# Layer 2's experts moved out of the attention loop, over the tokens that chose them

## The chip, the cores and the metric

The kernel runs on one core of a Trainium2 chip. Its time is the device time of one execution in microseconds, lower is better. Before the change the median of four runs is 3542.0 us (3536.94 to 3548.18).

## The reference, cut to what matters

Four layers, each a cross attention block and a feed-forward block with a residual around each, on x of 16 sequences of 256 tokens and 256 channels in float32. Layer 2's feed-forward block is what the change touches:

```python
x = x + L2_xattn(ctx, layernorm(x), kmask)
y = layernorm(x)                               # goes into L2_ffn
h = rms(y, n1_w); q, k = rms per head; v       # 16 heads of 16, causal
ao = causal_attention(q, k, v) @ wo.T;  ao[:, :, :64] = 0
y = y + ao
xf = rms(y, n2_w)
topv, topi = top_k(softmax(xf @ gate_w.T), 2)  # 4 experts, 2 for each token
topv = topv / (topv.sum() + 1e-8)
o0 = gelu(xf @ e0_up.T) @ e0_down.T
o1 = silu(xf @ e1_w1.T) * (xf @ e1_w2.T) @ e1_down.T
o2 = gelu(gelu(gelu(xf @ e2_l1.T) @ e2_l2.T) @ e2_l3.T) @ e2_l4.T
o3 = gelu(gelu(xf @ e3_down.T) @ e3_up.T) @ e3_out.T
moe = sum over the experts of weight * o;  moe[:, :, :64] = 0
x = x + (y + moe)
```

The hidden width is 512 (256 in e3_down). An expert's output counts only for the tokens that have it among their two.

## The kernel before, in words

The kernel walks the four layers one after the other. Layer 0 is a software-pipelined loop over 16 batches (a batch is one sequence), then experts over fixed slots of 512 tokens. Layer 1 is a gather loop, a shared expert and blocks of 256 tokens that belong to one expert each. Layer 2 is one pipelined loop that holds everything: cross attention, causal self-attention, routing, and all four experts over all tokens. Layer 3 is a pipelined loop with a cross attention and at its end a quantized product.

In the three pipelined loops the order of the work is written by hand, for TensorE (PE), VectorE (DVE), ScalarE (ACT) and GpSimd (POOL): a list `order` of entries (position, function, lag, arguments). At step s each entry is called, in order of position, for batch s - lag. All four engines take their instructions in this order, so an instruction that waits holds what stands behind it on its own engine. The DMA queue of SyncE (SP) is not ordered by the list; indirect DMAs (gathers and scatters by row numbers) are issued by POOL.

Layer 2's loop, for one batch b, with lines of the profile. `x_fetch` (L1212) gathers layer 1's expert outputs, `x_sum`, `x_norm` and `x_queries` make the queries; the cross attention is an object `Heads32` with `maxima` (scores on PE L223, maxima on DVE L305), `exps` (PE L242 and L245, four exponentials on ACT L252), `added` (POOL L338 adds the two key halves of the exponentials, to halve the sums on PE), `values` (PE L347, then reciprocal L355 and product L356 on DVE). `x_back` (L1239) adds to x; `statistics`, `norm`, `turned`, `project` (L1271, L1274), `head_squares` (L1286), `head_scale` (L1294) and `heads_q`, `heads_k` (L270, through transposes) make the inputs of the self-attention. `maxima` (PE L1308 for the causal mask and L223, DVE L1318) ends what a batch does in its own step. In the next step come `exps` (L245, ACT L252, then POOL L1327 sets to zero what the causal mask excludes), `values` (L261), `back` (L1344), `out_project` (L1357), `experts_in`, `gates` (L1385). One step later come `route` and `routed`, and the experts of the batch, cut in some 30 pieces that stand between the other entries of the order: `f_up` (PE L1454, two tokens' halves of 256 columns in one PSUM bank), its activations on ACT (L1466 gelu, L1471 tanh) and DVE (L1472, L1476), `f_down` (PE L1481, 192 columns), and `f_add` (DVE L1489), which adds each expert's output with a weight that is zero for tokens that did not choose it. The weights, 14 parts, are loaded anew for each batch through 7 buffers (`fetch`). PSUM has 8 banks: 4 for scores, 1 for transposes, 1 for attention outputs, 2 for experts.

Layer 3's loop does `prepare` (loads), `statistics`, `norm`, `turned`, `keys`, `vals`, `queries`, the cross attention (`maxima`, `exps`, `added`, `values` as above), `finish` (L1695) and `z_norm`. Layer 0's order has functions of its own; `load` there also zeroes DRAM buffers.

Of the kernel before, what the change touches and what calls it, by code (L numbers as in the profile page):

```python
# [19 lines left out]
P = 128  # L20
# [16 lines left out]
def tile_kernel(ctx: ExitStack, tc: tile.TileContext, a, out):  # L37
# [72 lines left out]
    yslots = keep.tile([NBLK * BLK, D], F32, name="yslots")  # L110
    idx1 = ct([P, 2, NT], "idx1", U32)
# [287 lines left out]
    with ExitStack() as l01:  # L399
# [30 lines left out]
        with ExitStack() as l0:  # L430
# [47 lines left out]
            def load(b):  # L478
# [10 lines left out]
                if 2 <= b < 6:  # L489
                    for k in range(2):  # L490
                        dma(xe[k][(b - 2) * 1024 : (b - 1) * 1024, :].rearrange("(p r) d -> p (r d)", p=P), zero)
                        if b == 2:
                            dma(ye[k][8 * CAP :, :], zero[0:1, :D])
                if 6 <= b < 6 + (NBLK * BLK + 1023) // 1024:
# [122 lines left out]
            def scatter(b, n):  # L617
# [17 lines left out]
                (0, exps, 0, 0), (1, q_stats, -2), (2, back, 1, 0), (3, maxima, -1, 1), (4, scatter, 3, 1),  # L635
                (5, back, 1, 1), (6, values, 0, 0), (7, t_stats, 1), (8, exps, 0, 1), (9, queries, -1, 0, QMs),
                (10, maxima, -1, 2), (11, slots, 2), (12, values, 0, 1), (13, t_norm, 1), (14, exps, 0, 2),
                (15, q_norm, -2), (16, scatter, 5, 4), (17, maxima, -1, 3), (18, turned, 1), (19, values, 0, 2),
                (20, queries, -2, 0, QTs), (21, exps, 0, 3), (22, router, 1), (23, maxima, -2, 0), (24, route, 1),
                (25, load, -3), (26, queries, -1, 1, QMs), (27, values, 0, 3), (28, queries, -2, 1, QTs),  # L640
                (29, scatter, 3, 2), (30, v_heads, -2),
# [476 lines left out]
    with ExitStack() as l2:  # L1118
# [6 lines left out]
        wts = t2([P, NT, 4], "wts")  # L1125


        with ExitStack() as l2a:
# [3 lines left out]
            psums(l2a, "ps2", 4, 1, 1)  # L1132
            pf2 = l2a.enter_context(tc.tile_pool(name="ps2_ffn", bufs=2, space=PSUM))
            fp = l2a.enter_context(tc.tile_pool(name="fp2", bufs=8))
# [8 lines left out]
            n2w = col(a["n2_w"], 2, "n2w", ca)  # L1143
# [17 lines left out]
            trif = ta([P, P], "trif")  # L1161
            V.memset(trif, 0.0)
            G.affine_select(trif, trif, [[-1, P]], ALU.is_ge, -MASKED, base=0, channel_multiplier=1)
            tri2 = ta([P, 2, P], "tri2", BF16)
            for i in range(2):
                V.tensor_copy(tri2[:, i, :], trif)
# [140 lines left out]
            def mask(sc, j, t):  # L1307
                T.matmul(  # L1308
                    sc[:, :, t * P : (t + 1) * P], lhsT=ident_bf, rhs=tri2,
                    start=True, stop=False, skip_group_check=True,  # L1310
                )

# [9 lines left out]
            def exps(b, u):  # L1322
                pT = pTs[b, u] = probs(u // 2, u % 2, QMs[b], KTs[b], 32, 0.0, 1.0, None, None, True)
                q0 = u % 2 * P

                for e in pT:
                    G.affine_select(  # L1327
                        e[:, :, q0 : q0 + P], e[:, :, q0 : q0 + P], [[0, 2], [1, P]], ALU.is_ge, 0.0, base=0, channel_multiplier=-1
                    )
# [21 lines left out]
            def out_project(b):  # L1351
                xn, ss = xcs.pop(b), small(2, "ss")
                hh = hhs[b, 1] = wp.tile([P, 2, D], F32, name="hh", tag="hh")
# [23 lines left out]
            def experts_in(b):  # L1377
                xfs[b] = wp.tile([P, 2, S], F32, name="xf", tag="xf")
                transposed(xfs[b], hhs.pop((b, 1)), n2w, A)

            def gates(b):
                p, xf = ptr(), xfs[b]
# [19 lines left out]

            def routed(b):

                pr, w, m = routes.pop(b), wts[:, 2 * b : 2 * b + 2, :], small(2, "rm")
# [3 lines left out]
                oh = [sm.tile([P, 2, 4], F32, name=f"oh2{k}", tag=f"oh2{k}", bufs=2) for k in range(2)]  # L1409
                m12 = [small(2, f"m12{k}", bufs=2) for k in range(2)]  # L1410
                top2(pr, 2, 4, oh, m12)
# [387 lines left out]
```

## Time and profile before

| | |
|---|---|
| median of four runs | 3542.0 us |
| profiled execution | 3548.84 us, span 3547.1 us, mean granted TensorE clock 0.928 |
| busy | PE 3149.2, DVE 1578.2, ACT 1162.8, POOL 1064.2 us |
| layer 0's loop | about 20 to 415 us |
| layer 0's experts | about 460 to 930 us |
| layer 2's loop | about 1690 us to its last store at 3059 us |
| one steady step of it | 80.7 us |
| layer 3's loop | about 3089 to 3460 us, one step 22.05 us |

The profile is one execution. Its page gives each engine's busy time, 40 equal slices of the span with the busy share in tenths and the granted TensorE clock (PEclk), and groups of instructions by line: busy time, mean duration in ns, and the engine's idle time just before them with the operation that ended most of it. PEld is the load of weights, which runs beside PE. The timeline lists instructions in order of time. L-numbers are lines of the kernel; where a helper issues the instruction, the line is the helper's.

### The profile page before, as it was taken

Reading aid. Unit: us, or ns where it says so; the run is one execution under the profiler, and the core shown is the slowest. Engines: PE = TensorE matmul, PEld = TensorE weight load, DVE = VectorE, ACT = ScalarE, POOL = GpSimd, SP = SyncE. Lnnn points to the kernel's source line nnn. Section 1 sums busy time; section 2 is a strip of 40 time slices with the busy share of each in tenths; the row PEclk is TensorE's granted clock in tenths of the full one; section 3 lists DMA queues with packets and bytes.
Section 4 is the critical chain, followed back from the end, with each engine's and each line's share of the span. In section 5 each row is a group of like instructions: output and inputs, shape, how many; then the busy total and the mean of one; then the engine's idle time right before and its main releaser. Section 6 shows DMA issues by size and latency. Waiting matters only on the chain. (4 is left out here: it accounts for less than half of the span.)

```text
span 3547.1 us, 54867 instructions
## 1 busy us (share of the span) xinstructions
PE 3149.2 (89%) x21640; PEld 2300.6 (65%) x21640; DVE 1578.2 (44%) x3920; ACT 1162.8 (33%) x2085; POOL 1064.2 (30%) x1643
## 2 busy tenths in 40 slices
PE   7999599999777489996689999999999999699983
PEld 4666366666565258885357777777777778567751
DVE  6766511100375222222445544454555542277766
ACT  3555221111122011111235545445554454122221
POOL 2455600000472600001233333333333222055552
PEclk8999799999888799997579999999999999899995
DMA  5411112221232336664013333333333223411101
GB/s 222 151 48 41 67 64 73 70 78 41 66 116 74 107 114 201 200 194 155 21 38 99 100 101 104 105 102 104 110 108 101 84 85 115 146 31 31 31 7 48
DMA packets 262132, 332.87 MB, mean 94 GB/s; under 512 B 20891, under 2 KB 214091, under 8 KB 259700
## 3 DMA queue, kind: packets, MB, share of 16 engines
q1 hardware_dynamic: 249588, 296.59, 26.2%
q0 software_dynamic: 12288, 32.78, 2.7%
q8 instruction: 171, 2.80, 0.3%
q14 instruction: 85, 0.70, 0.1%
HBM read 259.29 MB, written 70.80 MB: 93 GB/s over the span
## 5 line engine op out<-in xcount | busy, mean ns | idle before, releaser
L1454 PE MATMUL pf<-hf,fw 128*128 128x256 f32 x1280 | 302.5, 380 | 0.0
L1454 PE MATMUL pf<-xf,fw 128*128 128x256 f32 x1152 | 291.1, 390 | 0.0
L252 ACT ACTIVATE big<-pmm 128x512 f32<-128x512 f32 (+1 forms) x512 | 237.2, 549 | 124.5 <-PE pmm L245 116.1
L1454 PEld LDWEIGHTS pf<-hf,fw 128*128 128x128 f32 x1280 | 234.6, 190 | 31.8 <-issue 4.8
L1454 PEld LDWEIGHTS pf<-xf,fw 128*128 128x128 f32 x1152 | 208.0, 190 | 55.1 <-issue 27.6
L780 PE MATMUL pmm<-xiT,w 128*128 128x512 f32 x512 | 225.6, 599 | 5.5 <-DVE xiT L134 5.4
L788 PE MATMUL pacc<-w,h 128*128 128x256 f32 x1024 | 223.6, 379 | 0.0
L1327 POOL TENSOR_SCALAR_AFFINE_SELECT big<-big 128x256 f32<-128x256 f32 x256 | 105.0, 427 | 395.2 <-ACT big L252 388.4
L788 PEld LDWEIGHTS pacc<-w,h 128*128 128x128 f32 x1024 | 194.6, 190 | 33.3 <-issue 7.7
L816 POOL DMA_INDIRECT y<-ye,idx x64 | 65.2, 1019 | 479.3 <-issue 479.3
L789 DVE COPY yo<-pacc 128x256 f32<-128x256 f32 x64 | 27.2, 425 | 402.1 <-PE pacc L788 402.1
L305 DVE TENSOR_REDUCE max<-pmm 128x2 f32<-128x512 f32 x256 | 158.9, 682 | 91.6 <-PE pmm L223 91.1
L1481 PE MATMUL pf<-fw,hf 128*128 128x192 f32 x1024 | 191.2, 331 | 0.2
L1318 DVE TENSOR_REDUCE qpad<-pmm 128x2 f32<-128x256 f32 (+1 forms) x256 | 124.9, 551 | 139.7 <-PE pmm L223 139.7
L522 DVE TENSOR_REDUCE qpad<-pmm 128x2 f32<-128x512 f32 x256 | 159.0, 684 | 52.0 <-PE pmm L223 49.8
L338 POOL TENSOR_TENSOR big<-big 128x512 f32<-128x512 f32 x128 | 158.6, 1272 | 73.3 <-ACT big L252 73.2
L780 PEld LDWEIGHTS pmm<-xiT,w 128*128 128x128 f32 x512 | 96.3, 191 | 124.6 <-issue 112.4
L1481 PEld LDWEIGHTS pf<-fw,hf 128*128 128x128 f32 x1024 | 165.6, 190 | 13.7 <-issue 11.9
L1212 POOL DMA_INDIRECT y<-yslots,idx x64 | 66.7, 1042 | 319.5 <-DMA yslots<-yb 305.9
L355 DVE RECIPROCAL rT<-pacc 128x256 f32<-128x256 f32 x64 | 112.1, 1751 | 95.3 <-PE pacc L347 95.3
L1466 ACT ACTIVATE hf<-pf 128x512 f32<-128x512 f32 x176 | 104.8, 595 | 124.3 <-PE pf L1454 123.6
L146 POOL TENSOR_SCALAR rsq<-mv 128x2 f32<-128x2 f32 x128 | 25.1, 196 | 355.9 <-DVE mv L164 338.1
(383 smaller groups left out, 6213.1 us busy)
## 6 DMA issues: line engine op xcount, KB each, us to landing
w<-in_w_dram SPq DMA_DIRECT2D x16, 1024.0 KB
fw<-in_e_upT_dram SPq DMA_DIRECT2D x32, 512.0 KB
fw<-in_e_l2T_dram SPq DMA_DIRECT2D x32, 512.0 KB
fw<-in_e_l3T_dram SPq DMA_DIRECT2D x32, 512.0 KB
wg<-in_w_gate_dram SPq DMA_DIRECT2D x39, 352.0 KB
wu<-in_w_up_dram SPq DMA_DIRECT2D x39, 352.0 KB
fw<-in_e_downT_dram SPq DMA_DIRECT2D x32, 384.0 KB
wd<-in_w_down_dram SPq DMA_DIRECT2D x39, 256.0 KB
```

The lines of the kernel that those rows point to most:

```text
L252: A.activation(e[:, :, q0:], sc[j], AF.Exp, bias=bias, scale=scale)
L305: V.tensor_reduce(self.m[:, t, j, :], sc, AX.X, ALU.max, negate=True)
L338: G.tensor_tensor(r, self.pT[0][j], self.pT[1][j], ALU.add)
L355: V.reciprocal(rT, p[:, 1, :])
L522: V.tensor_reduce(qps[b][t][:, 8 * cp + j : 8 * cp + j + 5 : 4, 17], sc, AX.X, ALU.max, negate=True)
L780: T.matmul(p, lhsT=w1[:, c, f * P : (f + 1) * P], rhs=xiT[:, c, :], start=(c == 0), stop=(c == 1))
L788: T.matmul(p[:, :D], lhsT=hT[f][:, s * P : (s + 1) * P], rhs=w2[:, f, :], start=(f == 0), stop=(f == 7))
L1318: V.tensor_reduce(qp[:, 8 * cp + j : 8 * cp + j + 5 : 4, 16], sc, AX.X, ALU.max, negate=True)
L1327: G.affine_select(e[:, :, q0 : q0 + P], e[:, :, q0 : q0 + P], [[0, 2], [1, P]], ALU.is_ge, 0.0, base=0, channel_multiplier=-1)
L1454: T.matmul(p[:, j * S : (j + 1) * S], lhsT=w[:, c, f * P : (f + 1) * P], rhs=x, start=(c == 0), stop=(c == len(src) - 1),)
L1466: A.activation(f_hidden(to, f), p, AF.Gelu)
L1481: T.matmul(p[:, t * S : t * S + D - M], lhsT=hs[src][f // 2][:, f % 2, t * P : (t + 1) * P], rhs=w[:, f, :], start=(f == 0), stop=(f == 3),)
```

## The change

The experts leave layer 2's loop. In their place the loop does, for each batch: `routed` keeps the one-hot choices and the two weights; `places` counts, with two small matmuls and a running sum, at which row of its expert's region each token and choice goes; `scatter` writes the normalized token rows `hh` to these rows of a DRAM buffer `xe2` (four indirect DMAs on POOL a batch, a small memset ahead of each); `x_out` stores x without the experts' sum. After the loop each expert runs over its own region, 2048 rows in blocks of 512 (`tokens`); then, behind branches on the expert's count, over further blocks of 128, 128, 256, 512, 512 and 512 rows. The outputs go to a DRAM buffer `ye2`. Layer 3's loop gathers them (`fetch`, four indirect DMAs on POOL a batch) and adds them with their weights (`chosen`).

In the attention of layer 2, the causal mask of `exps` becomes a matmul ahead of the scores (`maskT`), instead of POOL's affine select after the exponential; the entries "added" are gone, so that `values` sums both halves on PE; scores have 5 PSUM banks instead of 4 and transposes 2 instead of 1, as the experts' 2 are free. The orders of the loops of layers 0, 2 and 3 are written anew; in layers 2 and 3, exps 0 of the cross attention moves from the start of a step to the end of the step before. Layer 0's `load` zeroes `xe2` and the upper half of each region of `ye2` as well.

```diff
+    REG = B * S
+    xe2 = keep.tile([4 * REG, D], F32, name="xe2")
+    ye2 = keep.tile([4 * REG, D - 64], F32, name="ye2")
...
+                dma(xe2[b * 1024 : (b + 1) * 1024, :].rearrange("(p r) d -> p (r d)", p=P), zero)
+                n0 = b // 4 * REG + REG // 2 + b % 4 * 512
+                dma(ye2[n0 : n0 + 512, :].rearrange("(p r) d -> p (r d)", p=P), zero[:, : 4 * (D - 64)])
...
-            psums(l2a, "ps2", 4, 1, 1)
-            pf2 = l2a.enter_context(tc.tile_pool(name="ps2_ffn", bufs=2, space=PSUM))
+            psums(l2a, "ps2", 5, 2, 1)
...
+            def maskT(sc):
+                T.matmul(sc[:, :, :P], lhsT=ident_bf, rhs=tri2[:, 1], start=True, stop=False, skip_group_check=True)
...
-                pT = pTs[b, u] = probs(u // 2, u % 2, QMs[b], KTs[b], 32, 0.0, 1.0, None, None, True)
-                q0 = u % 2 * P
-                for e in pT:
-                    G.affine_select(
-                        e[:, :, q0 : q0 + P], e[:, :, q0 : q0 + P], [[0, 2], [1, P]], ALU.is_ge, 0.0, base=0, channel_multiplier=-1
-                    )
+                pTs[b, u] = probs(u // 2, u % 2, QMs[b], KTs[b], 32, 0.0, 1.0, None, maskT, True)
...
+            def places(b):
+                oh = ohs.pop(b).rearrange("p t k e -> p (t k) e")
+                ohf = oh.rearrange("p a e -> p (a e)")
+                p = ptr()
+                T.matmul(p[:, 0:16], lhsT=before, rhs=ohf, start=True, stop=True)
+                T.matmul(p[:, 16:32], lhsT=ones, rhs=ohf, start=True, stop=True)
+                cum = sm.tile([P, 5, 4], F32, name="cumx", tag="cumx", bufs=2)
+                V.tensor_copy(cum[:, 0, :], taken[0])
+                for i in range(4):
+                    V.tensor_tensor(cum[:, i + 1, :], cum[:, i, :], p[:, 16 + 4 * i : 20 + 4 * i], ALU.add)
+                taken[0] = cum[:, 4, :]
...
+            def scatter(b, t):
+                for k in range(2):
+                    G.memset(apart, 0.0)
+                    i = G.indirect_dma_start(
+                        out=xe2, out_offset=bass.IndirectOffsetOnAxis(ap=idx2[:, k, 2 * b + t : 2 * b + t + 1], axis=0),
+                        in_=hhs[b, 1][:, t, :], in_offset=None,
+                    )
...
             order = [
+                (0, x_step, 0, "exps", 1), (1, heads_q, 1, 0, QMs), (2, gates, 2), (3, route, 2), (4, x_out, 2),
+                (5, weights, 1), (6, x_mask, -1), (7, x_step, 0, "values", 0), (8, routed, 2),
+                (9, x_step, 0, "values", 1), (10, heads_q, 1, 1, QMs), (11, exps, 1, 0), (12, x_load, -2),
+                (13, x_back, 0), (14, statistics, 0), (15, exps, 1, 1), (16, x_queries, -1), (17, x_fetch, -2, 0, 0),
+                (18, x_step, -1, "maxima", 0), (19, values, 1, 0), (20, norm, 0), (21, places, 2), (22, values, 1, 1),
+                (23, turned, 0), (24, x_step, -1, "maxima", 1), (25, x_step, -1, "split"), (26, project, 0, 0),
+                (27, x_fetch, -2, 0, 1), (28, project, 0, 1), (29, scatter, 2, 0), (30, head_squares, 0, 0),
+                (31, head_squares, 0, 1), (32, head_scale, 0), (33, exps, 1, 2), (34, exps, 1, 3),
+                (35, x_step, -1, "turned"), (36, values, 1, 2), (37, values, 1, 3), (38, heads_k, 0, 0),
+                (39, back, 1, 0), (40, back, 1, 1), (41, heads_q, 0, 0, QTs), (42, heads_k, 0, 1),
+                (43, heads_q, 0, 1, QTs), (44, maxima, 0, 0), (45, x_fetch, -2, 1, 0), (46, normed_again, 1),
+                (47, scatter, 2, 1), (48, back_turned, 1), (49, maxima, 0, 1), (50, out_project, 1), (51, maxima, 0, 2),
+                (52, maxima, 0, 3), (53, x_fetch, -2, 1, 1), (54, x_sum, -2), (55, x_norm, -2), (56, experts_in, 1),
+                (57, x_step, -1, "exps", 0),
             ]
...
+            def tokens(e, n0, n):
+                r, rows = n // P, slice(e * REG + n0, e * REG + n0 + n)
+                xi = fx.tile([P, 4, D], F32, name="xi2", tag="xi2", bufs=3)
+                dma(xi[:, :r, :], xe2[rows, :].rearrange("(p r) d -> p r d", r=r))
+                x = [fx.tile([P, 512], F32, name="xT2", tag="xT2", bufs=4) for c in range(2)]
+                for c in range(2):
+                    p = ptr()
+                    for i in range(r):
+                        T.transpose(p[:, i * P : (i + 1) * P], xi[:, i, c * P : (c + 1) * P], ident)
+                    evac(x[c][:, :n], p[:, :n], n2w[:, c : c + 1])
...
+                dma(ye2[rows, :].rearrange("(p r) d -> p r d", r=r), yo[:, :r, :])
+            share = REG // 2
+            for e in range(4):
+                for n0 in range(0, share, 512):
+                    tokens(e, n0, 512)
+            def more(e, many, n0, sizes):
+                if sizes:
+                    with tc.If(many > n0):
+                        tokens(e, n0, sizes[0])
+                        more(e, many, n0 + sizes[0], sizes[1:])
+            for e in range(4):
+                many = nc.values_load(cnt[0:1, e : e + 1], min_val=0, max_val=REG)
+                more(e, many, share, [128, 128, 256, 512, 512, 512])
...
+            (0, finish, 1, 0), (1, fetch, -4, 0, 0), (2, x_step, -1, "maxima", 0), (3, finish, 1, 1),
+            (4, x_step, 0, "exps", 1), (5, x_step, 0, "added", 1), (6, fetch, -4, 0, 1), (7, x_step, 0, "added", 2),
+            (8, x_step, 0, "added", 0), (9, x_step, 0, "added", 3), (10, statistics, -3), (11, statistics, 1),
...
+            (25, fetch, -4, 1, 1), (26, x_step, -1, "turned"), (27, vals, -2, 1), (28, mask_row, -3), (29, prepare, -4),
+            (30, chosen, -4), (31, x_step, -1, "exps", 0),
```

## The prediction

> **What bounds the kernel now.** I read the page first, its busy shares and its 40 slices.
>
> ```profile
> PE 3149.2 (89%) x21640; PEld 2300.6 (65%) x21640; DVE 1578.2 (44%) x3920; ACT 1162.8 (33%) x2085; POOL 1064.2 (30%) x1643
> PE   7999599999777489996689999999999999699983
> PEclk8999799999888799997579999999999999899995
> ```
>
> Slices 22 to 34 of 40 (about 1850 to 3000 us) are layer 2's loop: PE 9 everywhere, PEclk 9. So that stage is bound by TensorE at the full clock, and work taken off TensorE there counts if nothing takes its place. Next the windows of one steady step of this loop (80.7 us from one "turned" to the next), and of the step before experts have any token: step 1, which runs the same attention and no expert.
>
> ```profile
> 2201.50:2282.20 80.70, 79.89 (x648) 62.47 (x646) 41.35 (x112) 41.13 (x72) 27.04 (x47) 1.00 0.33 104
> 1746.70:1826.70 80.00, 63.66 (x430) 37.54 (x429) 36.03 (x79) 23.31 (x49) 27.50 (x46) 0.65 0.05 16
> ```
>
> Columns: length, busy PE, PEld, DVE, ACT, POOL, granted clock. This pair is the case in small: without experts the step took 80.0 us, no less than with them. They fill the holes of the attention, and without them the clock fell to 0.65. The timeline of step 1 shows the holes (in brackets, idle PE and what ended it):
>
> ```profile
> 1761.46 1.07 PE L347 MATMUL pacc<-big,ones 128*32 128x256 f32 x6 [2.66 <-POOL big L338]
> 1764.95 1.93 PE L347 MATMUL pacc<-big,val 128*32 128x256 f32 x16 [1.37 <-DVE uT L356]
> 1799.71 1.11 PE L270 MATMUL ptr<-ident,qpad 128*128 128x128 f32 x4 [0.78 <-ACT KT L141]
> ```
>
> They sum to about 17 us; most of the 80 is slow clock. Then the steady timeline, for true rates (start to start, since printed durations overlap):
>
> ```profile
> 2206.83 1.89 PE L1454 MATMUL pf<-hf,fw 128*128 128x256 f32 x8
> 2208.56 0.60 PE L270 MATMUL ptr<-ident,qpad 128*128 128x128 f32 x4
> 2221.49 1.46 PE L1481 MATMUL pf<-fw,hf 128*128 128x192 f32 x8
> 2222.79 0.60 PE L1308 MATMUL pmm<-tri,ident_bf 128*128 128x256 bf16 x4
> 2272.13 1.88 PE L1271 MATMUL pmm<-wqk,hT 128*128 128x512 f32 x4
> 2273.84 1.03 PE L1274 MATMUL pmm<-wvT,hT 128*128 128x256 f32 x4
> ```
>
> 256 columns cost 1.73/8 = 0.216 us, 192 columns 1.30/8 = 0.163, 512 columns 1.71/4 = 0.43: cost goes with columns, so wider blocks gain nothing on TensorE by themselves. Last the groups by shape, for the other engines' prices:
>
> ```profile
> L1327 POOL TENSOR_SCALAR_AFFINE_SELECT big<-big 128x256 f32<-128x256 f32 x236 | 96.4, 425 | 369.6 <-ACT big L252 363.5
> L1466 ACT ACT_TABLE_LOAD x59 | 75.7, 1283 | 6.5 <-PE pf L1454 5.7
> L1318 DVE TENSOR_REDUCE qpad<-pmm 128x2 f32<-128x512 f32 x112 | 69.6, 684 | 41.1 <-PE pmm L223 41.1
> L355 DVE RECIPROCAL rT<-pacc 128x256 f32<-128x256 f32 x26 | 45.6, 1754 | 49.6 <-PE pacc L347 49.6
> ```
>
> **Removed from the loop.** Per batch 152 expert matmuls of 256 columns and 64 of 192: 152 x 0.216 + 64 x 0.163 = 43.3 us of TensorE, of 80.7. ScalarE loses 11 gelus (0.595), 2 tanhs (0.613) and some 8 table loads (116 in the 1150 us of the groups, 1.283 each): 41.1 - 18.1 = 23 us left. POOL loses 16 affine selects (0.425) and 4 adds (1.275), and gains 4 scatters (as L1212's gathers, 1.05) and 4 memsets (about 0.13): 27 - 11.9 + 4.7 = 20. DVE loses f_add (8 x 0.407) and 4 x 0.681, and gains places, 11 small operations at some 0.18: 37. TensorE keeps 37.4 and gains 16 mask matmuls (4 in 0.53: 2.1) and 16 of ones32, since "added" is gone (8 in 0.54: 1.1): 41 us at full clock.
>
> **The new step.** No engine fills it, so the chain sets it: the order runs exps 1 of the cross attention (position 0) to maxima 3 (52) and exps 0 (57) of one batch in one step, and TensorE takes it in order. From the rows: exps 0 and 1 are 8 evictions on ScalarE, 0.688 each, values 0 done at 6.4; reciprocal 1.754, product 0.424, values 1 in the one pacc bank (1.8), the same DVE pair again: 13.2. x_back 0.43, add 0.69, statistics 1.2 on DVE and 3 on POOL, norm 0.9, turned, its eviction 0.94: 21.5. Two projections, 2.65 each: 26.8; their evictions, head_squares 0.69, head_scale's 12 small operations 2.9 and two products 1.15: 33. Six transposes through two banks that ScalarE or DVE drain (0.69): 37. Maxima: 8 x 0.418 + 8 x 0.684 + 0.56 on DVE: 47.3; exps 0 then: 48.3 us with all clocks full. TensorE would be busy 41/48 = 85%. What the clock does with that decides. The attention of layer 0 (100 to 400 us) is 93% busy at 0.97, the gather stage 950 to 1110 is 75% busy at 0.84, step 1 at 0.65. About 16 us of the chain are matmuls; with a sixth of the time at half clock they cost 3 more. I take 51 us a step; bounds are 41 (TensorE alone) and 80 (step 1 as it was).
>
> [...]
>
> Loop: steps 1 to 15 took 80 + 14 x 80.7 = 1210, now 15 x 51 = 765; step 0 about 7 less. Drain: 103 us from 2956 to the last store; now step 16 without new batches 28, step 17 (routing, places, four scatters in series) 20, landing and first load 10: 45 less.
>
> **Experts behind the loop.** The reference's routing gives 2366, 1754, 2006 and 2066 tokens to the four experts. 16 fixed blocks of 512: 608 matmuls at 0.43 + 512 at 0.163 = 347; transposes 16 x 0.87 = 14; the wait for xT's eviction after each block's transposes (about 0.7, as these are issued only after the block before) 11, tails 6: 378. Layer 0's experts, built alike, ran at 99% and clock 1.00 (500 to 900), so no more is added. Weights are loaded once instead of 16 times; that was hidden and counts nothing, and e2's and e3's land while e0 and e1 run (77 + 49 us of cover; without it some 20).
>
> **Branches.** Expert 0 runs 128, 128 and 256 more, expert 3 128. SP issues each load inside its branch behind the store of the body before, so bodies run in series: load 2, transposes, up, gelu, down and copy 5 to 7: 7 + 7 + 9 + 8 = 31. Counts and the entry, where each engine waits for all others, 6. About 10 jumps on TensorE's way; no row here shows a jump. Nearest are an instruction packet and a landing:
>
> ```profile
> q8 instruction: 171, 2.80, 0.3%
> 3059.39 2.01 DMA xd<-x
> ```
>
> 0.3% of 16 queues over 3547 us is 1.0 us a packet; a jump lies between 0 and 3 us; I take 1.5, as both a packet and a start are in it: 15. Sum 52, bounds 35 and 95.
>
> [...]
>
> **Layer 3.** Four gathers a step on POOL (1.05) and four multiply-adds on DVE (0.41). One gather stands between two of the adds for which values 0 waits already:
>
> ```profile
> 3318.31 4.96 POOL L338 TENSOR_TENSOR big<-big 128x512 f32<-128x512 f32 x4 [0.43 <-ACT big L252]
> 3323.32 0.62 PE L347 MATMUL pacc<-big,ones 128*32 128x256 f32 x2 [0.17 <-POOL big L338]
> ```
>
> So that wait grows by 1.0, 16 times: 16 us (0 if exps 0, now issued a step earlier, gives it back; 30 if DVE, 74% busy, also lags). The first batch gathers before its statistics: 8. Layer 0 is reordered and writes 23 MB more zeros; DMA has room (share 0.19 from 100 to 400): 0, plus or minus 8.
>
> **Sum.** -1210 + 765 - 7 - 45 + 378 + 52 + 16 + 8 = -43 us on 3548.8 (span 3547.1): 3506. The four runs have a median 6.8 lower, so I forecast 3499. Each microsecond of the step is 15; the sum is zero at 53.9.
>
> **Rivals.** *The clock takes the cover's place.* Without experts TensorE falls to half clock in the holes, as in step 1, and its 41 us stretch; above 53.9 us a step the change loses. At 58 it gives 3604, at 80 it would be 3934. For it: step 1's 0.65. Against: its transposes had one bank, its exps four, "added" made the 2.66 us hole; those are gone. *A tight loop.* The order hides more of the chain than I count, DVE (37) and TensorE (41) come near their bounds: 44 us, 3394. For it: layers 0 and 3 run 93 to 99% busy with such orders; against: one pacc bank and the serial head_scale. *A dear tail.* Branches and drain at their upper ends with the step as forecast: 3542 to 3560. The change does what it says: half the expert rows are left out by counts that the reference fixes.
>
> **Chances.** Forecast (49 to 53 us) 0.45, tight loop 0.16, clock 0.31, dear tail 0.08. Faster by over 0.2% (7 us, about what a measurement here can tell from none): 0.42 + 0.16 + 0.01 = 0.59; slower: 0.29 + 0.05 = 0.34; the rest, 0.07, within. The range reaches from 45 us a step (3409) to 59 (3619); the forecast's own case alone is 3469 to 3529.
>
> **What would show it.** Right: a step of 49 to 53 us, clock 0.85 to 0.95 in it, an expert stretch near 380 us at 1.00 without affine selects or table loads in the loop, 50 us of gappy work before layer 3, a layer 3 step near 23 us. Wrong: a loop clock under 0.75, an expert stretch over 410, or holes over 3 us at each branch.

## The result and the profile after

The changed kernel is slower by 0.4%: 3551.5 us against 3540.7 (medians of 39 and 60 runs), ratio 1.0038, 95% interval 1.0029 to 1.0048. The forecast was 3499 and "faster"; the sign was wrong. The profiled execution has a span of 3554.4 us, 7.3 more than before.

The page of the changed kernel, busy shares and slices as shown of before:

```profile
PE 2982.7 (84%) x20130; PEld 1979.7 (56%) x20130; DVE 1576.3 (44%) x3980; ACT 972.4 (27%) x1903; POOL 1019.8 (29%) x1517
PE   7999599999677399996788888888859998499983
PEclk9999799999888699997789999999979999799995
```

Layer 2's loop is now the slices 21 to 29, at PE 8 where it was 9. Then come the experts (slices 31 to 34, PE 9 and 8, 0.99 of the full clock in the windows below) and the branches with the start of layer 3 (PE 4). TensorE's busy time fell by 167 us, where the prediction's figures give 16 x (80.7 - 41) - 361 = 274 at the full clock: what is left in the loop ran more slowly (granted clock 0.91 over the 14 steps below).

The windows of the changed kernel, columns as in the prediction ("turned", from which steps are counted, is that of the cross attention: TensorE's transposes of nmp, L325 before and L331 after): the 14 steps from the second to the last "turned", one steady step, the fixed expert blocks, the branches, layer 3's loop.

```profile
1703.70:2494.60 790.90, 657.65 (x6457) 399.81 (x6455) 512.35 (x1457) 322.62 (x690) 268.39 (x458) 0.91 0.12 37
2158.40:2214.70 56.30, 46.85 (x471) 28.93 (x467) 36.95 (x107) 23.32 (x50) 20.10 (x34) 0.91 0.13 41
2624.10:2997.20 373.10, 366.20 (x1248) 213.27 (x1248) 40.85 (x64) 76.96 (x123) 0.00 (x0) 0.99 0.10 36
2997.20:3049.50 52.30, 26.55 (x122) 23.05 (x122) 3.16 (x8) 9.64 (x25) 0.00 (x0) 0.74 0.10 31
3103.60:3444.70 341.10, 325.77 (x2918) 225.48 (x2918) 265.06 (x554) 86.49 (x149) 232.50 (x262) 0.98 0.14 40
```

And of before, the same 14 steps and layer 3's loop:

```profile
1719.60:2847.00 1127.40, 1088.37 (x8660) 832.38 (x8661) 570.04 (x1521) 550.38 (x960) 366.98 (x630) 0.96 0.30 92
3110.00:3439.40 329.40, 320.70 (x2918) 223.69 (x2918) 242.83 (x501) 87.77 (x150) 182.50 (x214) 0.99 0.09 27
```

| Stretch | before | after | difference | forecast |
|---|---|---|---|---|
| start to the first "turned" of layer 2 | 1678.0 | 1668.1 | -9.9 | 0 |
| first to second "turned" (step 0) | 41.6 | 35.6 | -6.0 | -7 |
| the 14 steps to the last "turned" | 1127.4 | 790.9 | -336.5 | 14 x (51 - 80.7) = -416 |
| last "turned" to layer 3's first | 263.0 | 609.0 | +346.0 | -30 - 45 + 378 + 52 + 8 = +363 |
| layer 3's loop | 329.4 | 341.1 | +11.7 | +16 |
| to the end | 107.7 | 109.7 | +2.0 | 0 |

The differences sum to +7.3, the forecast to -44 (-43 in its own rounding). Everything but the 14 steps came out 28 us better than forecast; these came out 79 worse, 56.5 us a step over the 14 (55.6 in the steady ones) where 51 was forecast. So the question for the runs was what makes the step 55.6.

The timeline of TensorE in one step of the changed kernel, from the cross attention's exps (L248, L251) to its values (L353):

```profile
2174.59 0.51 PE L248 MATMUL pmm<-minus,sel 32*128 32x256 bf16 x2
2176.03 0.26 PE L248 MATMUL pmm<-minus,sel 32*128 32x256 bf16 x1 [0.33 <-DVE qpad L1340]
2178.04 0.28 PE L248 MATMUL pmm<-minus,sel 32*128 32x256 bf16 x1 [0.67 <-ACT big L258]
2179.20 1.24 PE L251 MATMUL pmm<-QTx,KTx 32*128 32x256 f32 x8
2183.98 1.94 PE L353 MATMUL pacc<-big,val 128*32 128x256 f32 x16
2190.06 1.07 PE L353 MATMUL pacc<-big,val 128*32 128x256 f32 x16 [2.43 <-DVE rm L1424]
```

Three things are to be seen. The same 16 matmuls of L353 take 1.94 us for values 0 and 1.07 for values 1: the first ran at half rate. The "minus" matmuls wait for a score bank (pmm), held by the maxima's reductions (qpad) and by the exps' own evictions (big); over the whole step, the stops of this kind that the timeline lists ahead of L248, L1327 and L1333 add up to 3.5 us (L1327 and L1333 are the mask's matmuls, whose inputs are constants). And values 1 waits for VectorE, whose small instructions of routed also stand ahead of values 1's own reciprocal. The half rate lasts from 2178.2 to 2188.4 (granted clock 0.50 there).

### The profile page after: what moved, and what is told of

It is laid out like the page before. It is cut to its first block, busy times and chain, and to the rows that moved or that the text cites. A ratio compares the mean times of both kernels' runs of the same rounds, so it can differ in the third digit from the quotient of the medians.

```text
span 3554.4 us, 51627 instructions
## 1 busy us (share of the span) xinstructions
PE 2982.7 (84%) x20130; PEld 1979.7 (56%) x20130; DVE 1576.3 (44%) x3980; ACT 972.4 (27%) x1903; POOL 1019.8 (29%) x1517
## 5 line engine op out<-in xcount | busy, mean ns | idle before, releaser
L825 POOL DMA_INDIRECT y<-ye,idx x64 | 65.5, 1023 | 479.2 <-issue 479.2
L1674 POOL DMA_INDIRECT y<-ye,idx x64 | 64.4, 1006 | 459.6 <-SPq L1580 446.4
L152 POOL TENSOR_SCALAR rsq<-mv 128x2 f32<-128x2 f32 x128 | 25.6, 200 | 450.6 <-DVE mv L170 444.5
L1568 DVE COPY yo<-pacc 128x384 f32<-128x384 f32 (+1 forms) x36 | 19.5, 541 | 303.7 <-PE pacc L1564 303.7
L267 PE MATMUL pacc<-big,vpad 128*32 128x256 f32 (+1 forms) x2048 | 133.0, 369 | 0.3
L229 PE MATMUL pmm<-kpad,QT 32*128 32x256 f32 x1024 | 125.4, 431 | 3.5 <-ACT big L258 1.8
L353 PE MATMUL pacc<-big,val 128*32 128x256 f32 x1024 | 91.6, 449 | 43.6 <-DVE rm L1424 33.8
L276 PE MATMUL ptr<-ident,qpad 128*128 128x128 f32 x512 | 94.8, 314 | 35.2 <-DVE qpad L179 20.3
L1545 ACT ACTIVATE h<-pmm 128x512 f32<-128x512 f32 (+2 forms) x122 | 67.4, 554 | 196.2 <-PE pmm L1538 196.0
L791 ACT ACTIVATE h<-pmm 128x512 f32<-128x512 f32 x128 | 76.4, 597 | 155.6 <-PE pmm L789 155.6
L276 PEld LDWEIGHTS ptr<-ident,qpad 128*128 128x128 f32 x512 | 61.6, 156 | 86.0 <-issue 48.9
```

The costliest lines, as they stand in the source:

```text
L229: T.matmul(sc[j][:, i, :nk], lhsT=QT[rows, c, t * P : (t + 1) * P], rhs=KT[rows, c, :nk], start=(mask is None), stop=True, skip_group_chec ...
L267: T.matmul(O[32 * j : 32 * j + 32, i, q0:], lhsT=lhsT(kc, 8 * cp + 4 * i + j), rhs=pT[j][:, i, q0:], start=(kc == 0 and i == 0), stop=(kc ...
L276: T.transpose(p[:, c, :], src[:, h0 + 4 * c : h0 + 4 * c + 4, :].rearrange("p h d -> p (h d)"), ident)
L353: T.matmul(p[32 * j : 32 * j + 32, k, :], lhsT=ones32 if k else self.val[:, kc, 32 * h : 32 * h + 32], rhs=self.sum[j][:, i, :] if k and s ...
L791: A.activation(h, p, AF.Gelu_apprx_tanh)
```

## The experiments

Two theories stood at the start. *Chain*: the step is one serial chain, and specific delays in it were left out. *Clock*: the granted clock (what grants it is "the gate" in two of the expectations) sets it, because the loop gives TensorE too little to do. A third, *engine work*, says that TensorE has more to do than was counted. The table has all runs. The step is the mean of the 14 from the second to the last "turned"; in brackets the median of the last 12 steps. The clock is that of those 14 steps. Steps and clock are of one profiled execution for each run. The ratio is to the kernel before in the same group of runs. The kernel before took 3460 us in some groups and 3545 in others; the 80 us lie ahead of layer 2 (first "turned" at 1590 or 1670), so only ratios and stretches are compared.

| Run | step, us | clock | layer 3 step | ratio [95%] |
|---|---|---|---|---|
| c_after (the changed kernel) | 55.8 (55.6) | 0.93 | 22.75 | 1.0038 [1.0026, 1.0050] |
| e1_routed | 57.1 (58.0) | 0.90 | 22.72 | 1.0078 [1.0050, 1.0106] |
| e3_between | 58.1 (57.9) | 0.88 | 22.74 | 1.0141 [1.0126, 1.0156] |
| e2_four | 66.1 (64.9) | 0.82 | 22.66 | 1.0516 [1.0500, 1.0531] |
| e2_warm | 63.1 (63.2) | 0.92 | 22.59 | 1.0371 [1.0356, 1.0387] |
| e9_six | 62.8 (63.1) | 0.86 | 22.65 | 1.0361 [1.0345, 1.0377] |
| e8_fill | 54.9 (54.6) | 0.99 | 22.66 | 0.9986 [0.9977, 0.9995] |
| e10_norm | 55.2 (54.5) | 0.98 | 22.75 | 0.9993 [0.9984, 1.0003] |
| e11_all | 55.7 (54.9) | 0.96 | 21.93 | 0.9969 [0.9958, 0.9981] |
| e12_less | 55.1 (54.6) | 0.96 | 21.96 | 0.9980 [0.9968, 0.9992] |
| e13_nofill | 56.7 (57.9) | 0.89 | 21.96 | 1.0024 [1.0010, 1.0038] |
| e14_early | 58.2 (59.1) | 0.86 | 22.67 | 1.0112 [1.0089, 1.0136] |
| e16_early_fill | 56.5 (57.2) | 0.96 | 22.68 | 1.0038 [1.0023, 1.0052] |
| e15_best | 59.3 (61.4) | 0.88 | 21.91 | 1.0200 [1.0181, 1.0219] |
| e17_all | 57.2 (56.3) | 0.91 | 21.88 | 1.0057 [1.0043, 1.0071] |
| e5_l3fetch | 55.8 (55.6) | 0.93 | 22.02 | 1.0018 [1.0001, 1.0036] |
| e18_fill_l3 | 54.7 (54.6) | 1.00 | 21.95 | 0.9950 [0.9937, 0.9964] |
| e7_before_noexp (one execution; it leaves out the experts' part of the result) | 76.5 (78.3) | 0.71 | 21.93 | - |

**The base and two changes of order.** The first is the changed kernel itself, the others move instructions.

Expected of c_after:

> The changed kernel itself, as the common base of this group of runs. All theories: layer 2's loop takes 55 to 56 us a step, and the ratio to the kernel before is 1.003 to 1.005. If the clock's windows set the step and not a chain of fixed length, a single execution may also hold stretches of steps of another length, such as the 58.0 us eight times in a row that the run with routed at 14.5 showed, and the ratio may then reach 1.01.

It came out as expected, 1.0038 again.

```diff
-(8, routed, 2),
+(14.5, routed, 2),
```

Expected of e1_routed:

> Layer 2's routed step is issued at 14.5 instead of 8, so that its small DVE instructions no longer stand ahead of the reciprocal of the cross attention's values 1. Chain theory (the step of 55.7 us is one serial chain, and routed holds it up there by the 1.2 us between the end of the values' matmuls and the reciprocal): the step falls by about 1.2 us, to 54.5, and the whole by some 19 us, to about 3533. Rival, engine work (the step grew because PE has more to do than was counted): no change within 0.1 us a step. Rival, clock (the slow stretch after the maxima sets the step, whatever DVE does): the reciprocal comes earlier, but the gain is lost again behind it, under 5 us in all.

The reciprocal did come earlier: x_back starts 15.6 us after exps 1 is issued instead of 17.3. But the stretch from there to "turned" grew from 20.3 to 23.7 us, with half rates in it. The chain theory's 1.2 us a step were lost again, and more. The last six steps are all of the same length (the expectation above miscounts them as eight); two of them:

```profile
2194.67:2252.70 58.03, 49.58 (x471) 29.80 (x467) 36.70 (x107) 23.20 (x50) 20.02 (x34) 0.88 0.13 40
2252.70:2310.73 58.03, 49.59 (x471) 29.80 (x467) 36.69 (x107) 23.32 (x50) 20.02 (x34) 0.88 0.11 35
```

The traces of before and of the changed kernel record the granted clock as 1.0 or 0.5, in 62 and 112 stretches. Each of these, the last of an execution aside, lasts a whole number of times 3.41 us, 1 to 359 times (such a length of 3.41 us is called a window here); 58.03 is 17 of them.

```diff
-(8, routed, 2), ... (10, heads_q, 1, 1, QMs), (11, exps, 1, 0),
+(14.5, routed, 2), ... (1.5, heads_q, 1, 1, QMs), (8, exps, 1, 0),
```

Expected of e3_between:

> As the run with routed at 14.5, and also the self-attention's queries (heads_q 1 of the step before) at 1.5 and its exps 0 at 8, between the values 0 and values 1 of the cross attention, so that PE has matmuls while values 1 waits for its bank and for DVE. Chain theory: exps 0 moves out of the stretch behind values 1 into a hole of 2.4 us, which takes 2 to 4 us off the step (52 to 54) and 30 to 60 us off the whole (3490 to 3520). Rival, engine work: PE's busy time is the same, so the step stays within 0.5 us of 55.7. A third way: the ACT evictions of exps 0 stand ahead of those that values 1 needs, and the step grows by 1 to 2 us.

A miss for both named theories; the third way had the sign. 57.9 us, clock 0.88. Against e1_routed, whose edit it holds, it is 1.0 us longer on the mean and no longer on the median.

**Banks, and added matmuls.** The changed loop has five banks for scores, two for transposes and one for the values.

```diff
-psums(l2a, "ps2", 5, 2, 1)
+psums(l2a, "ps2", 4, 2, 1)
```

Expected of e2_four:

> Layer 2's score banks go from 5 to 4; nothing else. It is the control for the run with added matmuls, which needs the eighth bank. Chain theory with the bank waits as one of its terms: the step grows by 0.5 to 2 us (8 to 32 us in all), since the exps of the cross attention wait for ACT to empty a bank more often. Rival, engine work: no change within 0.2 us a step.

One score bank less costs not 0.5 to 2 but some 10 us a step (7 in the next run, where added matmuls bring the clock to 0.92). That is the largest effect of any edit to the changed kernel here. The expectation of e9_six below gives 64.2 for this run; the table has 66.1. Next the same with added matmuls, which write only into the bank that came free:

```diff
+warm = ...tile([P, 512], F32, name="warm", tag="warm")
+def fill(b, n):
+    for _ in range(n):
+        T.matmul(warm, lhsT=ident_bf, rhs=tri2..., start=True, stop=True, ...)
+(49.5, fill, 0, 4), (51.5, fill, 0, 4), (52.5, fill, 0, 4), (56.5, fill, 0, 4), (0.5, fill, 1, 4), (7.5, fill, 1, 6),
```

Expected of e2_warm:

> As the run with 4 score banks, with 26 added bf16 matmuls of 128x512 a step in the eighth bank, whose results nobody reads, four or six each in the sparse maxima stretch at the step's end and at its start. They add about 26 x 0.22 = 5.5 us of PE work a step at full clock (0.22 estimated from the step's rows of bf16 matmuls of that width at full rate). Clock theory (the first 10 us of a step run at half rate because the maxima stretch before them leaves the array little to do): the matmuls of exps 1 and values 0 run at the full rate, and the step falls by 2 to 4 us against the run with 4 banks alone, although PE has more to do. Engine-work rival: the step grows by 3 to 6 us. If neither holds, the gate doesn't count this work, and the rates at the step's start stay at half.

The clock theory held: more work on TensorE, and the step fell by 3.0 us (1.7 on the median) while the clock rose from 0.82 to 0.92. Engine work as a cause is out. Then the other division of the banks, and the added matmuls with all banks kept:

```diff
-psums(l2a, "ps2", 5, 2, 1)
+psums(l2a, "ps2", 6, 1, 1)
```

Expected of e9_six:

> Six score banks and one transposes' bank in layer 2's loop, in place of five and two. The run with four and two took 64.2 us a step against 55.7. If the score banks are what the chain waits for, the sixth takes 1 to 4 us more off the step. Rival: the single bank of the transposes makes each wait for the eviction of the one before, about 0.6 us for some ten of them, and the step grows by 2 to 6 us. Clock theory: either way the step comes out near a multiple of 3.41 us.

The rival won: 62.8 us, so two banks for transposes matter as well. The split 5, 2, 1 is the best of the three.

```diff
+def fill(b, n):
+    p = pacc()
+    for _ in range(n):
+        T.matmul(p, lhsT=ident_bf, rhs=tri2..., start=True, stop=True, ...)
+(44.5, fill, 0, 4), (49.5, fill, 0, 4), (51.5, fill, 0, 4), (52.5, fill, 0, 4), (56.5, fill, 0, 4), (0.5, fill, 1, 4),
```

Expected of e8_fill:

> The changed kernel with all its banks, and 24 added bf16 matmuls of 128x512 a step, four each at six places between 44.5 and 0.5 of the order, into the bank of the values' sums, which stands free there. Nobody reads what they write. Clock theory: the stretch of exps 1 and values 0 runs at the full rate, the step falls by 2 to 4 us, to 52 to 54, and the whole by 30 to 60 us against the changed kernel, although PE has some 5 us more to do in each step. Engine-work rival: the step grows by 3 to 5 us. A third way: the clock is kept up where the work was added, and the half rate moves on into the projections, which leaves the step within 1 us of 55.7.

The windows of a step of this run, and its timeline at the place shown above:

```profile
2230.20:2284.80 54.60, 46.15 (x491) 28.92 (x490) 37.01 (x107) 23.20 (x50) 20.03 (x34) 1.00 0.12 38
```
```profile
2137.78 1.04 PE L1475 MATMUL pacc<-tri,ident_bf 128*128 128x512 bf16 x4
2139.09 1.03 PE L1475 MATMUL pacc<-tri,ident_bf 128*128 128x512 bf16 x4
2140.05 0.29 PE L248 MATMUL pmm<-minus,sel 32*128 32x256 bf16 x4
2142.09 0.26 PE L248 MATMUL pmm<-minus,sel 32*128 32x256 bf16 x1 [0.67 <-ACT big L258]
2143.25 0.71 PE L251 MATMUL pmm<-QTx,KTx 32*128 32x256 f32 x8
2146.63 1.07 PE L353 MATMUL pacc<-big,val 128*32 128x256 f32 x16
```

The clock is 1.00 and values 0 runs in 1.07 us. Yet the step is 54.6, only 1.0 less than in the changed kernel, where 2 to 4 were expected. From "turned" to exps 0 it is 19.0 us, against 16.2 in the changed kernel, since the added matmuls (L1475) stand there; from exps 0 to values 0 it is 6.6 against 9.4. What the clock gave, the added matmuls took. So at the full clock the chain lies between 54.6 - 2.8 = 51.8 and 54.6, and not at the 48.3 of the forecast. The granted clock gives the same lower end: three steady steps of the changed kernel (55.3, 55.6 and 56.3 us at 0.94, 0.94 and 0.91) hold seven windows of 3.41 us at half rate. These can have cost at most half their length, 3.98 us a step, and 55.74 - 3.98 = 51.8.

**Which term of the chain is too short?** At the full clock the segments of e8_fill stand against the forecast's: exps 0 to the end of values 0 8.5 (forecast 6.4), values 0 to x_back 6.8 (6.8), x_back to the projections 10.5 (8.3), the two projections 5.4 (5.3). Two of them are long by 2.1 and 2.2 us. The rest of the step, up to the next exps 0, is 23.4 against 21.5, and 20 of the 24 added matmuls stand in it. For the second, VectorE's timeline in e8_fill has the maxima's reductions ahead of norm (hh):

```profile
2161.05 2.48 DVE L311 TENSOR_REDUCE max<-pmm 128x2 f32<-128x512 f32 x4 [2.14 <-PE pmm L229]
2163.45 0.73 DVE L179 TENSOR_SCALAR hh<-x,mv,s 128x256 f32<-128x256 f32 x2
```

```diff
-(20, norm, 0), (21, places, 2),
+(17.5, norm, 0), (23.5, places, 2),
```

Expected of e10_norm:

> The run with the added matmuls (54.6 us a step, every matmul at the full rate), and norm at 17.5 instead of 20, ahead of the cross attention's maxima, and places at 23.5 instead of 21. Theory: at the full clock the step is a serial chain, and the forecast left out that DVE's four maxima reductions (2.49 us) stand ahead of norm's two instructions, which wait 1.6 us longer than for their own input: the step falls by 0.8 to 1.6 us, to 53.0 to 53.8. Rival (the step locks to the clock's windows of 3.41 us, of which 54.6 is 16): it stays at 54.6 or falls by a whole window to 51.2. Engine-work rival: no change, since no engine has less to do.

Nothing: 54.5 us. The same place in its timeline shows why:

```profile
2183.43 0.73 DVE L179 TENSOR_SCALAR hh<-x,mv,s 128x256 f32<-128x256 f32 x2 [2.98 <-POOL s L1266]
2186.02 0.37 PE L305 MATMUL pmm<-mb,ones_bf 1*128 1x512 bf16 x1 [0.23 <-DVE max L311]
2187.18 1.98 PE L1290 MATMUL pmm<-wqk,hT 128*128 128x512 f32 x4
```

norm now waits for its own input alone and starts 1.6 us earlier in the step (40.8 us after "turned" against 42.4). But the reductions start 1.5 us later, and the mask's matmul (L305), which stands ahead of the projections, waits for a bank that they hold. The projections start 0.3 us earlier than in e8_fill, and 0.1 of it is left at the end of the step.

Expected of e11_all:

> The same, with routed at 14.5 and layer 3's second gather behind its adds. Chain theory: now that the clock is full, the 1.2 us of DVE work ahead of values 1's reciprocal, which gave nothing at the slow clock, come off the step: 51.5 to 52.6 us a step, and layer 3 another 10 us less; in all some 40 us under the run with the added matmuls alone. Clock rival: as without the added matmuls, what is taken off comes back behind, and the step stays within 0.5 us of the run before it.

For e12_less, against e11_all:

```diff
-(52.5, fill, 0, 4), (56.5, fill, 0, 4),
+(52.5, fill, 0, 2), (56.5, fill, 0, 2),
```

Expected of e12_less:

> The same, with two instead of four added matmuls at each of the two places (52.5 and 56.5) that stand between maxima 3 and the cross attention's exps. Chain theory: 4 x 0.26 us less TensorE work on the chain, of which some is hidden behind the wait for a bank: 0.3 to 1.0 us a step less. Clock theory: if these are needed to hold the clock, half-rate matmuls return in exps 1 and values 0, and the step grows by 1 to 3 us.

Expected of e13_nofill:

> The run with all the changes of order, without any added matmul. Chain theory with the clock as a term of its own (about 4 us a step): 52 to 53 us a step, as 2 to 3 us of chain are gone, and about the time of the run with the added matmuls, which cost about as much on the chain as they save. Clock theory (what the chain loses, the gate takes back): 55 to 58 us a step, as with routed alone moved, where x_back came 1.7 us earlier and the step took 56 to 58.

None of the three is shorter than 54.6 us a step on the whole. e11_all lost the full clock (0.96) and its steps vary from 54.1 to 59.8; the two at clock 1.00 are 54.4 and 54.1, where the chain theory had 51.5 to 52.6. e12_less lost the full clock for 3.41 us in each steady step, and these are 54.6 each, 16 windows of 3.41. Of the last ten steps of e13_nofill, eight take 57.9 to 58.2 (17 windows) and two 54.7 (16). One of its early steps kept the full clock without any added matmul:

```profile
1819.34:1871.98 52.64, 43.88 (x470) 27.31 (x467) 36.21 (x104) 23.23 (x50) 18.26 (x32) 1.00 0.14 41
```

That is 1.5 to 1.8 us less than e11_all's two, which have the same order and the added matmuls, and still 4.3 over 48.3 (counted between other instructions, the step is 52.6 to 53.3). So the chain became a little shorter, but without added matmuls the run kept the full clock in this one step only.

For the first segment, exps 0 is moved ahead of maxima 3:

```diff
-(57, x_step, -1, "exps", 0),
+(51.5, x_step, -1, "exps", 0),
```

Expected of e14_early:

> The changed kernel with exps 0 of the cross attention at 51.5, between maxima 2 and maxima 3, instead of 57; nothing else. Its inputs are ready since 35. Chain theory (exps 0 to values 0 is on the chain, 2.1 us longer than forecast because of the banks): ScalarE evicts exps 0 while DVE reduces maxima 2 and 3, values 0 starts 2 to 3 us earlier after maxima 3, and the step falls to 52.5 to 54. Clock rival: the half rate moves to another place and the step comes out at 54.6 or at 58.0 (16 or 17 windows of 3.41 us). Rival on the banks: two more banks are taken between maxima 2 and maxima 3, which wait for them; what exps 0 gains maxima 3 loses, and the step stays within 0.7 us of 55.7.

Expected of e16_early_fill:

> The run with 24 added matmuls (54.6 us a step, all at the full rate) with exps 0 of the cross attention at 51.5; the four added matmuls that stood at 51.5 are at 51.2. At the full clock only the chain can answer. Chain theory: 2 to 3 us less, 51.5 to 52.6 a step. Rival on the banks: within 0.7 us of 54.6. Lock rival: exactly 54.6 again, or 51.2 (15 windows).

In e14_early the clock fell to 0.86 and the step came out at 58.2 (59.1), near the clock rival's 58.0 on the mean alone; its one step at the full clock is again shorter than those with added matmuls:

```profile
2230.72:2284.43 53.71, 43.54 (x470) 27.01 (x467) 36.79 (x107) 23.31 (x50) 20.07 (x34) 1.00 0.14 43
```

In e16_early_fill three of the 14 steps kept the full clock, and these are the test: 54.8 us, clock 1.00. Its timeline in one of them:

```profile
2233.15 0.26 PE L248 MATMUL pmm<-minus,sel 32*128 32x256 bf16 x1 [0.33 <-DVE qpad L1340]
2235.17 0.27 PE L1327 MATMUL pmm<-tri,ident_bf 128*128 128x256 bf16 x1 [0.54 <-ACT big L258]
2235.74 0.27 PE L1327 MATMUL pmm<-tri,ident_bf 128*128 128x256 bf16 x1 [0.31 <-ACT big L258]
2243.27 1.07 PE L353 MATMUL pacc<-big,val 128*32 128x256 f32 x16
```

exps 0 is done early, and now maxima 3 (L1327) waits for the banks that exps 0 holds. Values 0 starts 25.6 us after "turned" (2217.7), as in e8_fill (2146.63 - 2121.05). The rival on the banks won, on these three steps: from the maxima to the values the pace stays the same whichever stands first, and what stands second waits for the five score banks to be emptied.

Expected of e15_best:

> As the run before in this list, with 16 added matmuls a step (four each at 44.5, 49.5, 52.5 and 0.5), and layer 3's second gather behind its adds. Chain theory: the eight matmuls less are 2.1 us of TensorE work, of which at least 1 us stood on the chain, so 50.5 to 52 us a step if the clock holds; the whole about 1.5% faster than the kernel before. If the clock doesn't hold with 16, half rates come back and the step is 53 to 55.

Expected of e17_all:

> As the run before, with routed at 14.5, norm at 17.5 and places at 23.5. Chain theory: routed's 1.2 us come off the step on top (49.5 to 51), norm gives nothing by itself because the mask's matmul for the maxima then waits for a bank. Clock rival: as in the runs where routed was moved before, the gain is lost again to half rates between x_back and the projections: no less than the run before, or more.

Both missed. With 16 added matmuls the clock isn't held, 0.88 and 0.91: e15_best has three early steps of 54.83 at 1.00, no shorter than with 24, and it ends in eight steps of 61.44 us each, 18 windows of 3.41.

**The experts taken out, and nothing else.**

```diff
+work = []
...
-at_, scale = 0.5, 97.0 / sum(w[0] for w in work)
+at_, scale = 0.5, 0.0
...
-part(0, 0)
```

Expected of e7_before_noexp:

> The kernel before with layer 2's experts left out of its loop, and nothing in their place: the attention, the routing and the store of each batch in the order of before. It separates taking the experts out from writing the loop anew. The prediction read step 1 (80.0 us without experts, clock 0.65) as this loop's length without cover. If that holds, about 80 us a step, no less than with them. If step 1 was slow for a reason of its own (the loop's start), 55 to 65 us a step at a clock of 0.75 to 0.9, which is what a plain removal gives before any new order.

One step of it, from the windows:

```profile
2250.00:2328.30 78.30, 61.62 (x472) 36.95 (x465) 39.53 (x107) 24.89 (x55) 29.96 (x54) 0.71 0.08 23
```

76.5 us a step on the mean at clock 0.71: the 43.3 us of removed matmuls bring 4 us of 80.5. The other 20 us of the loop's gain come from the new order, the banks that the experts gave back, and the masks that left POOL, which were not separated. The prediction's reading of step 1 (80.0) came near, and it is what speaks most plainly against the change. Its first reading, that the stage is bound by TensorE and that work taken off it counts, was not borne out: with all of that work gone, and nothing in its place, the loop kept 95% of its time.

**Layer 3, and a version that beats both.**

```diff
-(6, fetch, -4, 0, 1),
+(9.5, fetch, -4, 0, 1),
```

Expected of e5_l3fetch:

> In layer 3, the second gather of the block four ahead (fetch -4, 0, 1) stands behind the four adds, at 9.5, instead of between the first and the second. The prediction's term for it was 1.0 us a step. If that term is right, layer 3's loop falls from 22.74 us a step by 0.6 to 1.0 us, 9 to 16 us in all. Rival: POOL's gathers don't bound the loop and the longer step comes from chosen's instructions on DVE: no change within 0.2 us a step.

The loop fell by 0.73 us a step, 11 in all: the prediction's mechanism for this stage was right, and nearly all of the stage's loss comes from that one gather.

Expected of e18_fill_l3:

> The changed kernel with the 24 added matmuls at their first places (54.6 us a step) and layer 3's second gather behind its adds (about 11 us in all), and no other change. If the terms add, as they lie in different stages: 54.6 us a step, 22.0 us a step in layer 3, ratio to the kernel before 0.995 to 0.997. If the clock falls into another pattern of windows, steps of 55 to 56 and a ratio near 1.000.

Both terms add. All 13 later steps are 54.6 us at clock 1.00. Ratio 0.9950, interval 0.9937 to 0.9964: faster than before by 0.5%, and than the changed kernel by 0.9% (0.9950/1.0038).

## Why the prediction was wrong

- **The step.** This is the step of the prediction that failed: "48.3 us with all clocks full", and with it 51. Measured at the full clock it is 54.6 with the added matmuls, at least 51.8 without; the single steps at 1.00 without them are 52.6 and 53.7, in orders slightly changed. The sum counted each instruction's duration and, for the order, who waits for whom; it counted no wait for a score bank. It named the one pacc bank and the two transposes' banks, but not the five score banks. The runs point to these as the place: one bank less costs 10 us, two moves of instructions (e10, e16) turned into waits for banks at the full clock, to within 0.3 us of the same step, and the listed waits for them are 3.5 us in the step shown of the changed kernel and 2.7 in one of e8_fill. That VectorE's reductions and ScalarE's evictions hold these banks is seen in the waits (0.33 us on qpad, 0.67 on big in the step shown). No run gave the scores a bank more without taking one from the transposes, so the length without this limit is not shown, nor that the banks account for all of the difference. The sum has slips too: its printed terms up to the end of the second DVE pair give 12.6 and not 13.2, its terms for the maxima 9.4 and not 10.3. They make the forecast longer, so the miss doesn't come from them.
- **The clock.** The allowance was 3 us; the changed kernel's clock share lies between 55.6 - 54.6 = 1.0 and 55.6 - 51.8 = 3.8. So the term was about right, and the loop's clock (0.91) is inside the forecast 0.85 to 0.95.
- **The rival "the clock takes the cover's place"** had the number (above 53.9) and half of the mechanism. The clock did fall in the sparse stretch (0.50 from 2178.2 to 2188.4 in the step shown), and 24 matmuls that compute nothing brought it back (0.99 in e8_fill). But at clock 1.00 the step is still above 53.9. What I had not priced is that the clock also hinders mending: shorter chains came out at 54.6, 58.0 or 61.4 us (e12_less, e1_routed, e15_best), 16, 17 or 18 windows.
- **Engine loads.** DVE 37, ACT 23, POOL 20 a step: measured 37.0, 23.3, 20.1. TensorE 41 at the full clock: 43.5 and 43.9 in the two steps at 1.00 without added matmuls. Near, and of little use, as no engine bounds the step.
- **Experts, branches.** 373 against 378 for the blocks, at clock 0.99; 52.3 against 52 for the branches. The other 12 of the -17 of that stretch lie in the drain and in layer 3's start, and were not followed up. In the branches the longest stop of TensorE is ahead of expert 3's body:

```profile
3038.72 0.66 PE L1532 MATMUL ptr<-ident,xi 128*128 128x128 f32 x2 [12.79 <-DMA xi<-xe]
```

  It holds, in series, the end of the body before, the jumps over the blocks that don't run, and the load; the prediction summed these one by one (2 us a load, 1.5 a jump), and how much of the stop each has was not read. No run shows a jump by itself, so its 1.5 us stays an estimate: the trace has 9.25 us from the issue of the last store before this body (3026.56) to the issue of its load (3035.81), the jumps among them, and 2.91 from there to the transposes.
- **Layer 3.** +0.78 us a step against 1.0; e5_l3fetch put 0.73 of it on the gather between the adds.
- **Ahead of layer 2.** -9.9 against 0. Kernels of this series with the same code up to there and the slower start came to the first "turned" between 1666.1 and 1675.3 us, so it may be no more than scatter; e7_before_noexp, with before's code up to there, came at 1595.9, and e18_fill_l3 in the same group at 1591.3.

With 56.5 instead of 51 in the sum, 14 steps cost 77 us more, and before's own steps were 80.5 on the mean and not 80.7 (2 us): -44 becomes +35. The 28 us that the other stretches came out better leave the measured +7. Of these 28 at least the 9.9 ahead of layer 2 and the 12 that were not followed up are no merit of the sum: that the whole missed by less than its step did is in good part luck. The profiled execution had somewhat longer early steps (61.8 and 58.5) than the base run (54.3 to 57.9), which is why its 14 steps are 56.5 and not 55.8.

## What to carry to other kernels

Price a serial step in banks as well as in instructions: count how many buffers the chain passes through, and who empties each, because the wait can move along with what is put first: in e16_early_fill exps 0 stood first, maxima 3 waited 0.54 and 0.31 us for its banks, and values 0 started 25.6 us after "turned", as in e8_fill. When dense work is taken out of a loop, look in the trace for a step that already ran without it; its length is the nearest row there is. Where the clock falls in a sparse stretch, added matmuls that write to a free bank are a cheap test of how much is the clock (e8_fill: 0.93 to 0.99, 55.8 us a step to 54.9), and sometimes worth keeping.

## What the runs showed of the hardware

All but the last of the 62 stretches of one granted clock in the trace of before, and of the 112 of the changed kernel, are whole multiples of 3.41 us. Three runs repeated a step near such a multiple: 58.03 us six times in a row in e1_routed (17.00), 61.44 eight times in e15_best (18.00), 54.6 ten times in e12_less (16.00). In e8_fill the step is 54.59, with the clock at 1.00 over the last 13 steps; that it is near 16 windows may be chance. In the changed kernel three steps together (55.3, 56.3, 55.6) make 49 windows. An edit meant to take 1.2 us off the chain cost 2.4 in e1_routed (58.0 against 55.6). The runs show the pattern; why a step repeats at such a length was not settled.

In the step shown of the changed kernel the clock fell (0.91) although TensorE was busy 46.85 of 56.3 us with no listed stop over 2.43; in the 3.4 us before the half rate begins at 2178.2, TensorE was busy 2.07 us, with 26 matmuls that use 32 of the 128 rows (32*128). With 24 bf16 matmuls of 128 rows and 512 columns a step it was 0.99 in e8_fill and 1.00 in e18_fill_l3, in other orders 0.98 (e10_norm) and 0.96 (e11_all, e16_early_fill); with 16, at other places and in another order, 0.88 and 0.91 (e15_best, e17_all). What decides it was not settled.
